# Layer 0's values by conjugate symmetry (264 real columns for 512), and layer 1 rebuilt with packed, transposed k

## The chip, the cores and the metric

The kernel runs on one core of one Trainium2 chip. A core has a matrix engine (PE, with its weight loads shown apart as PEld), a vector engine (DVE), an activation engine (ACT), a general engine (POOL) and queues for DMA; each works through its own instructions in its own order, and semaphores tie them together. The metric is device time in microseconds (us), the median of several runs. A matmul keeps one operand (the weights, `lhsT`) in the array and streams the columns of the other; a float32 matmul shows as two passes in the trace, each with its own weight load.

## The reference, cut to what matters

The input is 8 images of 256 channels, 96 x 96 pixels. Two layers follow each other, each added to its own input after a group norm (`_gn`).

```python
# layer 0: 8 heads of 32 channels
q_f, k_f, v_f = fft2(W1 x + b1), fft2(W2 x + b2), fft2(W3 x + b3)
q_f, k_f = l2_normalize(q_f), l2_normalize(k_f)
attn = einsum('bhcn,bhdn->bhcd', q_f, k_f) * temperature
attn = complex(softmax(real(attn)), softmax(imag(attn)))
out = abs(ifft2(einsum('bhcd,bhdn->bhcn', attn, v_f)))
x = x + W_out out
# layer 1: linear attention, d = 32
q = softplus(Wq xf + bq);  k = softplus(Wk xf + bk);  v = Wv xf + bv
attn_map = einsum('bdn,ben->bde', k, v)
k_sum = sum_n k + 1e-6
out = einsum('bnd,bde,bn->ben', q, attn_map, 1 / einsum('bnd,bd->bn', q, k_sum))
x = x + out
```

In the kernel the attention, the 2D transforms and W3 of layer 0 are folded together: each image row h is multiplied by a small complex matrix per batch (`mz`), giving a complex value z per pixel and channel, and then by a table T of the row (`tmat`, constant), giving a complex y whose absolute value is what W_out is applied to.

## The kernel before, in words

The eight images (batches) go one after the other. A batch's x is four tiles of 128 partitions x 2 halves of channels x 2304 pixels (24 rows each), taken from a pool of eight such buffers; the same pool gives layer 0's result `rs` (four) and layer 1's `kq` and `ex`. One tile framework records the instructions in program order: every engine keeps that order, and each wait comes from a buffer or a datum. PSUM is split into six banks handed round in a ring (`psum`, `ps_tile`, L70) and two more for sums that stay (`pacc`).

The stages of a batch:

- Statistics of x (`bn_stats`, L148, called at L494), then `group_norm` (L153) and the scaled weights.
- The q and k products of layer 0 (L235, L238), 72 chunks of 128 pixels, with squares on ACT (L243), their sum on POOL (L244) and the logits (L220); then softmax and the table `mz` (L268 to L306), 512 columns wide: 256 real and 256 imaginary parts.
- The z loop (L330 to L345), over 96 rows in pairs (`TR` = 2). For a row, PE makes z (two matmuls of 512 columns, L338), DVE adds the bias row (`zt`, L341), and `column` (L311) of the row before follows: four T products of 192 columns (L316, L318) into one PSUM bank, ACT squares them (L321), DVE adds the squares of real and imaginary parts (L322), and after the second row of a pair ACT takes four roots (L326) into `rs`. T's rows come by a DMA for each pair (L334) on the SP queue.
- W_out (`po`, L356), added to x on DVE (L358), with the statistics of layer 1.
- Layer 1: `kq` (L390) makes k and q for 384 pixels of all four x tiles at once, the four tiles in the four column groups of the array (32 outputs each), so that one PSUM bank holds four tiles' values and the order is half outside, tile inside. Softplus (L177) is Abs, Exp and Ln on ACT with DVE steps between.
- The sums of k and x: for 18 steps i, eight transposes of x (L420), two evictions (L425 on ACT, L427 on DVE), one transpose of k (L429, evicted by ACT at L430), and four `kx` matmuls (L408), one for each x tile, in the four column groups again. Then small matmuls make the table `am` (L443 to L460).
- The output (L463 to L488): for each of six slices of 384 pixels a denominator (L466), its reciprocal (L468, DVE) and a product (L469, POOL), made one slice ahead; then for each half of the channels four `o` matmuls (L481), one for each x tile, with 32 rows of weights each in the four row groups, and four adds to x (L484). An output DMA of 384 KB goes out for each tile and slice (L486). The next batch's x comes by four DMAs: two at the start of layer 1 (L383), one after the sums (L439), and one after the output (L488), since a buffer must be free for each.

Of the kernel before, what the change touches and what calls it, by code (L numbers as in the profile page):

```python
# [25 lines left out]
F32 = mybir.dt.float32  # L27
# [4 lines left out]
P = 128  # L32
KC = 2
# [4 lines left out]
TR = 2  # L38
GN_EPS = 1e-5
# [5 lines left out]
def two_layer_kernel(ctx: ExitStack, tc: tile.TileContext, x, w1t, b1, w2t, b2, w3, b3, wot, temp,  # L45
# [8 lines left out]
    SW = 768  # L54
    NS = TW // CH
    XW = XR * W
    assert C == KC * P and NT == 4 and TW % CH == 0 and XW % P == 0 and TW % SW == 0 and SW % P == 0 and ROWS % TR == 0
# [6 lines left out]
    psum = ctx.enter_context(tc.tile_pool(name="psum", bufs=6, space=bass.MemoryType.PSUM))  # L64
# [25 lines left out]
    e0blk = const.tile([P, P], F32, name="e0blk")  # L90
    nc.vector.memset(e0blk, 0.0)
    for j in range(4):
        s = slice(32 * j, 32 * j + 32)
        nc.vector.memset(hblk[s, s], 1.0)
        nc.vector.memset(e0blk[s, 32 * j:32 * j + 1], 1.0 / HEAD)
    rep4 = const.tile([P, P], F32, name="rep4")
    nc.vector.reduce_sum(rep4[:, 0:D], ident.rearrange("p (j d) -> p d j", d=D), axis=AX.X)
    for j in range(1, 4):
        nc.vector.tensor_copy(rep4[:, 32 * j:32 * j + 32], rep4[:, 0:D])
    xT = const.tile([P, 4, 2, C + 2], F32, name="xT")  # L100
    nc.vector.memset(xT, 1.0)
# [3 lines left out]
    nc.scalar.dma_start(out=gri, in_=gmat)  # L105
    epsb = const.tile([P, 1], F32, name="epsb")
# [8 lines left out]
    nc.scalar.dma_start(out=wo, in_=wot.rearrange("(k p) o -> p k o", p=P))  # L115
# [10 lines left out]
    nc.scalar.dma_start(out=bvrow, in_=bv.partition_broadcast(P))  # L126
    b3col = const.tile([P, KC], F32, name="b3col")
    for k in range(KC):
        nc.scalar.dma_start(out=b3col[:, k:k + 1], in_=b3[k * P:(k + 1) * P].unsqueeze(1))
    bkq4 = const.tile([P, 2], F32, name="bkq4")  # L130
    for j in range(4):
        nc.scalar.dma_start(out=bkq4[32 * j:32 * j + 32, 0:1], in_=bk.unsqueeze(1))
        nc.scalar.dma_start(out=bkq4[32 * j:32 * j + 32, 1:2], in_=bq.unsqueeze(1))
# [43 lines left out]
    def softplus(z, e, name):  # L177

        u = two.tile([P, SW], F32, tag="xf", name=f"spu_{name}")
        nc.vector.tensor_scalar_add(u, e, 1.0)  # L180
        nc.vector.scalar_tensor_tensor(e, in0=u, scalar=1.0, in1=e, op0=ALU.subtract, op1=ALU.subtract)
        nc.scalar.activation(u, u, AF.Ln)
        nc.vector.tensor_sub(u, u, e)
        nc.vector.scalar_tensor_tensor(z, in0=z, scalar=0.0, in1=u, op0=ALU.max, op1=ALU.add)  # L184
# [17 lines left out]
    def layer0(b, st0):  # L202
# [13 lines left out]
        lg = [pacc.tile([P, 512], F32, tag="acc", name=f"lg{m}_{b}") for m in range(KC)]  # L216
# [51 lines left out]
        mz = one.tile([P, KC, 2 * C], F32, tag="wbig", name=f"mz_{b}")  # L268
        pz = ps_tile(f"zb_{b}")
        for m in range(KC):  # L270
# [16 lines left out]
            nc.tensor.matmul(pa[:, 0:2 * P], lhsT=sbd, rhs=gri, start=True, stop=True)  # L287
            at = one.tile([P, 2, P], F32, tag="at", name=f"at_{b}_{m}")
            nc.scalar.copy(at[:, 0, :], pa[:, 0:P])
            nc.vector.tensor_add(at[:, 1, :], e0blk, pa[:, P:2 * P])  # L290
            for c in range(2):
                cols = slice(c * C + m * P, c * C + (m + 1) * P)
                nc.tensor.matmul(pz[:, cols], lhsT=b3b[:, m, :], rhs=at[:, c, :], start=True, stop=True)
            for k in range(KC):
                pm = ps_tile(f"mz_{b}_{m}_{k}")
                nc.tensor.matmul(pm[:, 0:2 * P], lhsT=w3n[:, m, k * P:(k + 1) * P],
                                 rhs=at.rearrange("p c o -> p (c o)"), start=True, stop=True)
                for c in range(2):
                    nc.vector.tensor_scalar_mul(mz[:, k, c * C + m * P:c * C + (m + 1) * P],
                                                pm[:, c * P:(c + 1) * P], rstd[:, k:k + 1])  # L300
        zrow = one.tile([P, 2 * C], F32, tag="row", name=f"zrow_{b}")
        nc.scalar.copy(zrow, pz)
        pn = ps_tile(f"zm_{b}")
        for k in range(KC):
            nc.tensor.matmul(pn, lhsT=nmb[:, k, :], rhs=mz[:, k, :], start=(k == 0), stop=(k == KC - 1))
        nc.vector.tensor_add(zrow, zrow, pn)  # L306
# [4 lines left out]
        def column(h, zt, tm, s2):  # L311
            hl = h % TR
            py = ps_tile(f"y_{b}_{h}")
            for m in range(KC):
                o = slice(m * 2 * W, (m + 1) * 2 * W)
                nc.tensor.matmul(py[:, o], lhsT=zt[:, m * P:(m + 1) * P], rhs=tm[:, hl, W:3 * W],  # L316
                                 start=True, stop=False)
                nc.tensor.matmul(py[:, o], lhsT=zt[:, C + m * P:C + (m + 1) * P], rhs=tm[:, hl, 0:2 * W],  # L318
                                 start=False, stop=True)
            sq = two.tile([P, KC, 2, W], F32, tag="sq", name=f"ysq_{b}_{h}")  # L320
            nc.scalar.activation(sq.rearrange("p m c w -> p (m c w)"), py[:, 0:KC * 2 * W], AF.Square)  # L321
            nc.vector.tensor_add(s2[:, :, :, hl], sq[:, :, 0, :], sq[:, :, 1, :])  # L322
            if hl == TR - 1:
                for g in range(NT):
                    r4 = rs[g].rearrange("p k (h w) -> p k h w", w=W)
                    nc.scalar.activation(r4[:, :, :, h - TR + 1:h + 1],  # L326
                                         s2[:, :, g * ROWS:(g + 1) * ROWS, :], AF.Sqrt)

        pending = None
        for h in range(H):  # L330
            g, hl = divmod(h, ROWS)
            if h % TR == 0:
                tm = two.tile([W, TR, 3 * W], F32, tag="xf", name=f"tm_{b}_{h}")
                nc.sync.dma_start(out=tm, in_=tmat[:, h:h + TR, :])  # L334
                s2 = two.tile([P, KC, W, TR], F32, tag="s2", name=f"s2_{b}_{h}")
            ps = ps_tile(f"z_{b}_{h}")
            for k in range(KC):
                nc.tensor.matmul(ps[0:W, :], lhsT=xs[b][g][:, k, hl * W:(hl + 1) * W], rhs=mz[:, k, :],  # L338
                                 start=(k == 0), stop=(k == KC - 1))
            zt = three.tile([W, 2 * C], F32, tag="qk", name=f"zt_{b}_{h}")  # L340
            nc.vector.tensor_add(zt, zrow[0:W, :], ps[0:W, :])  # L341
            if pending is not None:
                column(*pending)
            pending = (h, zt, tm, s2)
# [17 lines left out]
    def layer1(b, st1):  # L362
        nmean, rstd, nmb = group_norm(st1, f"b{b}")
        wkq = one.tile([P, KC, 2, 4, D], F32, tag="row", name=f"wkq_{b}")
        wvs = one.tile([P, KC, C], F32, tag="wbig", name=f"wvs_{b}")
        for k in range(KC):
            for c, w in enumerate((wk, wq)):
                nc.vector.tensor_scalar_mul(wkq[:, k, c], w[:, k, :].unsqueeze(1).to_broadcast([P, 4, D]),
                                            rstd[:, k:k + 1])
            nc.vector.tensor_scalar_mul(wvs[:, k, :], wv[:, k, :], rstd[:, k:k + 1])  # L370
        pb = ps_tile(f"l1b_{b}")
        for c in range(2):
            for k in range(KC):
                nc.tensor.matmul(pb[:, C + c:C + c + 1], lhsT=wkq[:, k, c], rhs=nmean[:, k:k + 1],
                                 start=(k == 0), stop=(k == KC - 1))
# [171 lines left out]
```

## Time and profile before

| what | value |
|---|---|
| median of 3 runs | 5337.23 us (5336.09 to 5342.2) |
| profiled execution | 5342.2 us, span in the trace 5340.2 us |
| PE, DVE, ACT, POOL busy | 4945.2, 2533.8, 1402.8, 966.2 us |
| a batch (second: from its bias row to that of the next) | 714.57 to 1379.19, 664.6 us |
| of it: q, k products, softmax, `mz` | 714.57 to 895.40, 180.8 us |
| z loop | 895.40 to 1186.66, 291.3 us |
| `po`, group norm, layer 1's weights | 1186.66 to 1259.85, 73.2 us |
| in the first batch: k, q columns and sums | 594.8 to 648.4, 53.6 us |
| its output | 652.33 to 692.71, 40.4 us |

A profile row names the line, the engine, the operation, output and inputs, the count, the busy time and the mean length of one in ns, and the time for which the engine was idle before such an instruction, with what ended it. Busy times are summed for each engine and overlap between engines, so that what bounds a stage is read from that stage alone: from the chain of waits, and from the timeline in which starts repeat. The clock column (PEclk) is the share of full speed that PE was granted. Some costly rows:

```profile
L338 PE MATMUL z<-mz,x 128*96 128x512 f32 x3072 | 1444.0, 592 | 0.0
L341 DVE TENSOR_TENSOR zt<-zrow,z 96x512 f32<-96x512 f32 x768 | 524.7, 683 | 599.3 <-PE z L338 599.3
L321 ACT ACTIVATE ysq<-y 128x384 f32<-128x384 f32 x768 | 376.3, 490 | 1498.2 <-PE y L318 1498.2
L148 DVE BATCH_NORM_STATS2 st<-x 128x6 f32<-128x384 f32 x768 | 393.5, 554 | 51.9 <-DMA x<-in_x_dram 45.9
```

ACT's wait for y in the z loop (1498.2 us in all) shows that it has room there; DVE's waits for z say the same.

### The profile page before, as it was taken

The numbers are of one execution on the slowest core, as the hardware profiler recorded it, in microseconds if no ns is written. First come the engines' busy times: TensorE is split into PE (matmuls) and PEld (weight loads), VectorE is DVE, ScalarE is ACT, GpSimd is POOL, SyncE is SP. The second block draws the span as 40 slices with busy tenths as digits, with TensorE's granted clock in tenths as the row PEclk, the third lists the DMA queues.
The fourth block names the chain that finished last, engine by engine and source line by source line (L and its number), as shares of the span: only waits on it lengthen the run. The fifth ranks groups of instructions, "written<-read, shape, count | busy, mean of one in ns | idle before, by whom it ended". The sixth has DMA issues, their size and how long they took to land.

```text
span 5340.2 us, 61775 instructions
## 1 busy us (share of the span) xinstructions
PE 4945.2 (93%) x23024; PEld 3423.1 (64%) x23024; DVE 2533.8 (47%) x4724; ACT 1402.8 (26%) x3576; POOL 966.2 (18%) x1102
## 2 busy tenths in 40 slices
PE   6999989999899998999989999899998999889998
PEld 5766567665676647766477664776647766476664
DVE  4333843338433484334843348433483334833347
ACT  1222212222122221222222222222222222222222
POOL 4400044000430005300053000530005300052000
PEclk9999989998899988999889998899988999899997
DMA  2011120111101111011110112101121011200101
GB/s 86 12 37 32 66 77 13 38 31 71 72 14 37 36 72 66 16 37 47 71 54 17 38 45 74 51 17 37 45 83 42 19 37 56 82 30 21 37 24 72
DMA packets 107914, 241.89 MB, mean 45 GB/s; under 512 B 11488, under 2 KB 62560, under 8 KB 99424
## 3 DMA queue, kind: packets, MB, share of 16 engines
q1 hardware_dynamic: 103936, 235.97, 13.3%
q8 instruction: 184, 3.01, 0.2%
q10 hardware_dynamic: 3680, 1.97, 0.1%
q14 instruction: 114, 0.93, 0.1%
HBM read 162.40 MB, written 75.50 MB: 45 GB/s over the span
## 4 chain that ended last, share of the span: by engine, by line
PE 88%; DVE 6%; ACT 3%; DMA 2%; issue 1%; POOL 0%; SPq 0%; ACTq 0%; DVEq 0%; POOLq 0%
PE z L338 25%; PE qk L235 9%; PE y L316 9%; PE y L318 9%; PE qk L238 9%; PE po L356 9%; PE lg L220 5%; PE o L481 3%; PE xT L420 3%; DVE st L148 2%; PE kx L408 2%; DMA x<-in_x_dram 1%; PE kq L390 1%; DVE x L484 1%; PE den L466 1%
## 5 line engine op out<-in xcount | busy, mean ns | idle before, releaser
L338 PE MATMUL z<-mz,x 128*96 128x512 f32 x3072 | 1444.0, 592 | 0.0
L244 POOL TENSOR_TENSOR acc<-acc,sq 128x512 f32<-128x512 f32 x576 | 730.3, 1268 | 477.2 <-ACT sq L243 474.9
L341 DVE TENSOR_TENSOR zt<-zrow,z 96x512 f32<-96x512 f32 x768 | 524.7, 683 | 599.3 <-PE z L338 599.3
L316 PEld LDWEIGHTS y<-tm,zt 96*128 96x128 f32 x3072 | 562.5, 190 | 384.4 <-issue 380.1
L241 DVE TENSOR_TENSOR qks<-brow,qk 128x512 f32<-128x512 f32 x576 | 396.2, 688 | 851.8 <-PE qk L238 851.8
L321 ACT ACTIVATE ysq<-y 128x384 f32<-128x384 f32 x768 | 376.3, 490 | 1498.2 <-PE y L318 1498.2
L338 PEld LDWEIGHTS z<-mz,x 128*96 128x96 f32 x3072 | 499.6, 163 | 419.6 <-issue 417.7
L316 PE MATMUL y<-tm,zt 96*128 96x192 f32 x3072 | 751.2, 326 | 0.0
L318 PE MATMUL y<-tm,zt 96*128 96x192 f32 x3072 | 748.8, 325 | 0.0
L322 DVE TENSOR_TENSOR s<-ysq 128x192 f32<-128x192 f32 x768 | 277.2, 361 | 919.6 <-ACT ysq L321 919.6
L243 ACT ACTIVATE sq<-qks 128x512 f32<-128x512 f32 x576 | 363.5, 631 | 931.5 <-DVE qks L241 929.7
L235 PE MATMUL qk<-w12s,x 128*128 128x256 f32 x2304 | 594.8, 381 | 0.0
L238 PE MATMUL qk<-w12s,xf 128*128 128x256 f32 x2304 | 592.1, 379 | 0.0
L318 PEld LDWEIGHTS y<-tm,zt 96*128 96x128 f32 x3072 | 539.2, 189 | 0.0
L194 POOL COPY xf<-x 128x190 f32<-128x190 f32 x32 | 10.9, 342 | 2866.4 <-DVE kq L184 2858.7
L356 PE MATMUL po<-r,wo 128*128 128x384 f32 x1536 | 497.5, 487 | 10.8 <-ACT r L326 10.8
L238 PEld LDWEIGHTS qk<-w12s,xf 128*128 128x128 f32 x2304 | 438.7, 190 | 60.0
L356 PEld LDWEIGHTS po<-r,wo 128*128 128x128 f32 x1536 | 291.2, 190 | 214.6 <-ACT r L326 13.2
L235 PEld LDWEIGHTS qk<-w12s,x 128*128 128x128 f32 x2304 | 397.3, 192 | 37.9 <-issue 7.5
L148 DVE BATCH_NORM_STATS2 st<-x 128x6 f32<-128x384 f32 x768 | 393.5, 554 | 51.9 <-DMA x<-in_x_dram 45.9
L220 PEld LDWEIGHTS lg<-qks 128*128 128x128 f32 x2304 | 347.1, 191 | 34.1 <-DVE qks L241 4.8
L220 PE MATMUL lg<-qks 128*128 128x128 f32 x2304 | 350.8, 275 | 3.2 <-DVE qks L241 3.2
(140 smaller groups left out, 3367.4 us busy)
## 6 DMA issues: line engine op xcount, KB each, us to landing
tm<-in_tmat_dram SPq DMA_DIRECT2D x384, 216.0 KB, 2.6
x<-in_x_dram SPq DMA_DIRECT2D x32, 2304.0 KB, 8.1
out_dram<-x SPq DMA_DIRECT2D x192, 384.0 KB, 3.7
w<-in_w1t_dram ACTq DMA_DIRECT2D x1, 256.0 KB, 8.6
w<-in_w2t_dram ACTq DMA_DIRECT2D x1, 256.0 KB, 8.9
w3n<-in_w_dram ACTq DMA_DIRECT2D x1, 256.0 KB, 9.0
wo<-in_wot_dram ACTq DMA_DIRECT2D x1, 256.0 KB, 9.2
wv<-in_wvt_dram ACTq DMA_DIRECT2D x1, 256.0 KB, 9.6
```

The costliest lines, as they stand in the source:

```text
L148: nc.vector.bn_stats(out=st[:, k, g * NS + s, :], in_=xt[:, k, s * CH:(s + 1) * CH])
L220: nc.tensor.matmul(lg[m][:, 0:P], lhsT=qk[:, m * P:(m + 1) * P], rhs=qk[:, C + m * P:C + (m + 1) * P], start=(i == 0), stop=(i == NT * NI ...
L235: nc.tensor.matmul(ps[:, 0:C], lhsT=xg[:, k, n], rhs=w12s[:, k, 0:C], start=(k == 0), stop=(k == KC - 1))
L238: nc.tensor.matmul(ps[:, C:2 * C], lhsT=xf[:, k, nf], rhs=w12s[:, k, C:2 * C], start=(k == 0), stop=(k == KC - 1))
L241: nc.vector.tensor_add(qk, brow, ps)
L244: nc.gpsimd.tensor_add(acc, acc, sq)
L316: nc.tensor.matmul(py[:, o], lhsT=zt[:, m * P:(m + 1) * P], rhs=tm[:, hl, W:3 * W], start=True, stop=False)
L318: nc.tensor.matmul(py[:, o], lhsT=zt[:, C + m * P:C + (m + 1) * P], rhs=tm[:, hl, 0:2 * W], start=False, stop=True)
L321: nc.scalar.activation(sq.rearrange("p m c w -> p (m c w)"), py[:, 0:KC * 2 * W], AF.Square)
L338: nc.tensor.matmul(ps[0:W, :], lhsT=xs[b][g][:, k, hl * W:(hl + 1) * W], rhs=mz[:, k, :], start=(k == 0), stop=(k == KC - 1))
L341: nc.vector.tensor_add(zt, zrow[0:W, :], ps[0:W, :])
L356: nc.tensor.matmul(po[:, 0:CH], lhsT=wo[:, k, m * P:(m + 1) * P], rhs=rs[g][:, k, n], start=(k == 0), stop=(k == KC - 1))
```

## The change

Layer 0: the values of a head's channels are conjugates of each other in pairs, n and 32 - n, so that 17 of 32 channels determine all. `mz` gets 33 x 8 = 264 real columns (17 real and 16 imaginary parts of channel values times 8 heads) for 512. A row then needs three T products instead of four: of the first 128 columns with the one part of T, of the second 128 with the turned part, and of 8 columns (the channels that have no partner) apart. The sum and the difference of the first two give the pair's two values; so there is a copy by ACT (`yb`), an add and a subtraction by DVE (`yc`), a square of 768 values by ACT, a square of 8 x 384 (`x2`), two adds on POOL and the four roots, all once for a pair of rows. `wo` is loaded in the matching order of channels by 32 small DMAs on SP.

PSUM: the ring has four banks instead of six, and the staying tiles have two banks each instead of one.

Layer 1: k is made pixel by pixel (`k_group`: 12 chunks of 128 pixels as weights, 32 columns streamed), q as before but with the tile outside and the half inside (`q_chunk`); the sums go over 72 chunks of 128 pixels (`kx_group`), each with two transposes, one eviction on DVE, and one matmul into the same 32 rows. The softplus takes 384 columns at a time. `wvs` and `bvs` are gone: the scale goes into `kxT`. Output: all six denominators first, then tile by tile, one DMA of a whole x tile (2304 KB) for each. Layer 1 holds one x buffer instead of two, so that three loads of the next x are issued at its start and the fourth after the first output tile.

```diff
+NZ = 33
+NH = 8
-    psum = ctx.enter_context(tc.tile_pool(name="psum", bufs=6, space=bass.MemoryType.PSUM))
+    psum = ctx.enter_context(tc.tile_pool(name="psum", bufs=4, space=bass.MemoryType.PSUM))
     pacc = ctx.enter_context(tc.tile_pool(name="pacc", bufs=2, space=bass.MemoryType.PSUM))
...
-    nc.scalar.dma_start(out=wo, in_=wot.rearrange("(k p) o -> p k o", p=P))
+    wo_v = wot.rearrange("(n q) o -> q n o", q=HEAD)
+    for j in range(16):
+        for k in range(KC):
+            c = (j, HEAD - j if j else 16)[k]
+            nc.sync.dma_start(out=wo[8 * j:8 * j + 8, k, :], in_=wo_v[c])
...
-    def softplus(z, e, name):
-        u = two.tile([P, SW], F32, tag="xf", name=f"spu_{name}")
+    def softplus(dst, z, name):
+        e = two.tile([P, CH], F32, tag="sq", name=f"spe_{name}")
+        nc.scalar.activation(e, z, AF.Abs)
+        nc.scalar.activation(e, e, AF.Exp, scale=-1.0)
+        u = two.tile([P, CH], F32, tag="s2", name=f"spu_{name}")
...
-            sq = two.tile([P, KC, 2, W], F32, tag="sq", name=f"ysq_{b}_{h}")
-            nc.scalar.activation(sq.rearrange("p m c w -> p (m c w)"), py[:, 0:KC * 2 * W], AF.Square)
-            nc.vector.tensor_add(s2[:, :, :, hl], sq[:, :, 0, :], sq[:, :, 1, :])
+            real, turned = tm[:, hl, W:3 * W], tm[:, hl, 0:2 * W]
+            nc.tensor.matmul(py[:, hl, 0:2 * W], lhsT=zt[:, 0:P], rhs=real, start=True, stop=True)
+            nc.tensor.matmul(py[:, hl, 2 * W:4 * W], lhsT=zt[:, P:2 * P], rhs=turned, start=True, stop=True)
+            nc.tensor.matmul(px[0:NH, hl * 2 * W:(hl + 1) * 2 * W], lhsT=zt[:, 2 * P:2 * P + NH], rhs=real,
+                             start=True, stop=True)
+            if hl < TR - 1:
+                return
+            yb = two.tile([P, TR, 2 * W], F32, tag="sq", name=f"yb_{b}_{h}")
+            nc.scalar.copy(yb, py[:, :, 2 * W:4 * W])
+            yc = two.tile([P, KC, TR, 2 * W], F32, tag="xf", name=f"yc_{b}_{h}")
+            nc.vector.tensor_add(yc[:, 0], py[:, :, 0:2 * W], yb)
+            nc.vector.tensor_sub(yc[:, 1], py[:, :, 0:2 * W], yb)
+            x2 = one.tile([NH, TR, 2 * W], F32, tag="x2", name=f"x2_{b}_{h}")
+            nc.scalar.activation(x2.rearrange("p t w -> p (t w)"), px[0:NH, 0:TR * 2 * W], AF.Square)
+            yf = yc.rearrange("p k t w -> p (k t w)")
+            nc.scalar.activation(yf, yf, AF.Square)
+            s2 = two.tile([P, KC, W, TR], F32, tag="s2", name=f"s2_{b}_{h}")
+            s2t = s2.rearrange("p k w t -> p k t w")
+            nc.gpsimd.tensor_add(s2t, yc[:, :, :, 0:W], yc[:, :, :, W:2 * W])
+            nc.gpsimd.tensor_add(s2t[0:NH, 1], x2[:, :, 0:W], x2[:, :, W:2 * W])
+            for g in range(NT):
+                r4 = rs[g].rearrange("p k (h w) -> p k h w", w=W)
+                nc.scalar.activation(r4[:, :, :, h - TR + 1:h + 1], s2[:, :, g * ROWS:(g + 1) * ROWS, :], AF.Sqrt)
...
-            zt = three.tile([W, 2 * C], F32, tag="qk", name=f"zt_{b}_{h}")
+            zt = three.tile([W, NZ * NH], F32, tag="qk", name=f"zt_{b}_{h}")
...
-        kq = x_tile(f"kq_{b}")
-        ex = x_tile(f"ex_{b}")
+        qp = x_tile(f"qp_{b}").rearrange("p k n -> p (k n)")
         if b + 1 < B:
-            xs[b + 1] = [load_x(b + 1, g) for g in range(NT - 2)]
+            xs[b + 1] = [load_x(b + 1, g) for g in range(NT - 1)]
...
+        def q_chunk(s):
+            n = slice(s * CH, (s + 1) * CH)
+            ps = ps_tile(f"q_{b}_{s}")
+            for j in range(NT):
+                for k in range(KC):
+                    nc.tensor.matmul(ps[32 * j:32 * j + 32, 0:CH], lhsT=wq4s[:, k, j, :],
+                                     rhs=xs[b][j][:, k, n], start=(k == 0), stop=(k == KC - 1))
+            z = three.tile([P, CH], F32, tag="qk", name=f"zq_{b}_{s}")
+            nc.vector.tensor_scalar_add(z, ps[:, 0:CH], bqs)
+            softplus(qp[:, n], z, f"q{b}_{s}")
...
+        def k_group(t):
+            ps = ps_tile(f"k_{b}_{t}")
+            for i in range(KG):
+                for k in range(KC):
+                    nc.tensor.matmul(ps[:, i * D:(i + 1) * D], lhsT=x_chunk(t * KG + i, k), rhs=wks[:, k, :],
+                                     start=(k == 0), stop=(k == KC - 1))
+            z = three.tile([P, KG, D], F32, tag="qk", name=f"zk_{b}_{t}")
+            nc.vector.tensor_add(z, ps[:, 0:KG * D].rearrange("p (i d) -> p i d", d=D),
+                                 bks.unsqueeze(1).to_broadcast([P, KG, D]))
+            sp = two.tile([P, KG * D], F32, tag="xf", name=f"spk_{b}_{t}")
+            softplus(sp, z.rearrange("p i d -> p (i d)"), f"k{b}_{t}")
+            return sp
...
+        def kx_group(t, ks):
+            pend = None
+            for c in range(t * KG, (t + 1) * KG):
+                pt = ps_tile(f"xT_{b}_{c}")
+                for k in range(KC):
+                    nc.tensor.transpose(pt[:, k * P:(k + 1) * P], x_chunk(c, k), ident)
+                xt = three.tile([P, C + 1], F32, tag="qk", name=f"xt_{b}_{c}")
+                nc.gpsimd.memset(xt[:, C:C + 1], 1.0)
+                nc.vector.tensor_add(xt[:, 0:C], nmrow, pt[:, 0:C])
+                if pend is not None:
+                    add_kx(*pend)
+                pend = (ks, c, xt)
+            add_kx(*pend)
         pend = None
-        for t in range(TW // SW):
...
+        for t in range(NG):
+            ks = k_group(t)
+            q_chunk(t)
+            if pend is not None:
+                kx_group(*pend)
+            pend = (t, ks)
+        kx_group(*pend)
...
-        normalize(0)
-        for s in range(NS):
...
+        for g in range(NT):
+            xg = xs[b][g]
+            jj = slice(32 * g, 32 * g + 32)
+            for s in range(NS):
+                n = slice(s * CH, (s + 1) * CH)
+                for m in range(KC):
+                    ps = ps_tile(f"o_{b}_{g}_{s}_{m}")
+                    nc.tensor.matmul(ps[:, 0:CH], lhsT=am[jj, m * P:(m + 1) * P], rhs=qp[jj, n],
+                                     start=True, stop=True)
+                    nc.vector.tensor_add(xg[:, m, n], xg[:, m, n], ps[:, 0:CH])
+            nc.sync.dma_start(out=out_v[b, :, :, g * TW:(g + 1) * TW], in_=xg)
+            if g == 0 and b + 1 < B:
+                xs[b + 1].append(load_x(b + 1, NT - 1))
```

## The prediction

> **What bounds the kernel now.** I read the page's shares first, then the chain that ended last, the costliest groups, the windows by stage, and the timeline where the change lands. The chain says TensorE: 88% of the span, z and y (L316, L318, L338) alone 43%.
>
> ```profile
> PE 4945.2 (93%) x23024; PEld 3423.1 (64%) x23024; DVE 2533.8 (47%) x4724; ACT 1402.8 (26%) x3576; POOL 966.2 (18%) x1102
> PE 88%; DVE 6%; ACT 3%; DMA 2%; issue 1%; POOL 0%; SPq 0%; ACTq 0%; DVEq 0%; POOLq 0%
> ```
>
> The z loop's timeline (start, length, engine) shows how it goes:
>
> ```profile
> 319.56 1.88 PE L338 MATMUL z<-mz,x 128*96 128x512 f32 x4
> 319.82 0.49 ACT L321 ACTIVATE ysq<-y 128x384 f32<-128x384 f32 x1 [1.30 <-PE y L318]
> 320.34 0.36 DVE L322 TENSOR_TENSOR s<-ysq 128x192 f32<-128x192 f32 x1 [1.20 <-ACT ysq L321]
> 322.57 1.88 PE L338 MATMUL z<-mz,x 128*96 128x512 f32 x4
> 323.75 0.80 ACT L326 ACTIVATE r<-s 128x96 f32<-128x96 f32 x4 [0.43 <-DVE s L322]
> ```
>
> z starts repeat every 3.01 us (322.57 - 319.56): a row. Passes follow each other without a gap, and all other engines wait for PE. So cutting columns pays there, until another engine's work per row is longer. Windows by stage of one batch (PE, PEld, DVE, ACT, POOL busy; then clock, DMA share, GB/s):
>
> ```profile
> 595.00:612.00 17.00, 17.00 (x186) 6.32 (x179) 10.56 (x17) 14.16 (x22) 0.00 (x0) 0.92 0.01 1
> 612.00:649.00 37.00, 33.12 (x309) 21.18 (x307) 28.00 (x40) 22.93 (x51) 0.47 (x2) 0.95 0.01 1
> 656.00:693.00 37.00, 35.41 (x104) 18.20 (x104) 33.88 (x54) 0.00 (x0) 5.01 (x6) 0.50 0.59 214
> 693.00:715.00 22.00, 1.60 (x5) 1.43 (x6) 14.21 (x35) 0.26 (x1) 1.68 (x4) 0.50 0.48 178
> ```
>
> The k and q columns take 17 us, layer 1's sums 37, its output 37. In the output the clock is 0.50 all through, though PE is busy, and DVE is nearly full too. Last, the stretch with no PE work is in the chain:
>
> ```profile
> 694.68 9.60 DMA x<-in_x_dram
> 704.30 5.62 DVE st L148 x12
> ```
>
> The next batch's last x tile is waited for.
>
> **What the Trainium skill says.** "TensorE: Matmul & The Clock Gate", LDWEIGHTS: a weight load takes its columns over 1.2, 107 ns for 128, however few columns are then streamed. The trace agrees: eight transposes of 128 columns start to end in 1.09 us. The same page, Why this matters for your kernels: a matmul of 32 rows takes as long as one of 128, and gains only by running beside others on other row or column groups. The trace has that too: eight kx passes of 257 columns, four groups side by side, take 0.64 us together. The same page, Part 1: an idle window of about 3.4 us halves the clock and a busy one restores it. The first half agrees (0.50 after the reciprocals); the second doesn't hold for the output's 32-row matmuls here, 37 us at 0.50. The same page, Architectural detail: ACT and DVE take their instructions strictly in order; the z loop below rests on that.
>
> **The change part by part** (per batch; there are eight). Durations from the profiled execution: 5342.2 us, span 5340.2; the median of the runs is 5337.23, 5.0 below.
>
> 1. *z loop.* PE: a row had z 2 x 512 and y 4 x 192 columns, 1792 in all for 3.01 us. It has 2 x 264 and 3 x 192, 1104: 1.85 us, 3.71 a pair. If PE stayed the bound, 48 pairs would take 178 instead of 291.3 us (895.40 to 1186.66 in the chain). But the rest is now one chain, from the copy of a pair to that of the next, since ACT holds yb, x2, the square, four roots, then the next yb, in this order:
>  - ACT yb, 128x384 out of PSUM: 0.49 (row L321), hop 0.09 (above, ACT's end at 320.31 to DVE's start is 0.03; from DVE to POOL at the reciprocals 0.14; I take values between);
>  - DVE add and sub of 384 with PSUM: 1.02 (two of 0.46 to 0.55, rows L358 and L484);
>  - ACT square of 768 in SBUF: 0.85 (row L182), hops 0.09;
>  - POOL add of 384: 1.00 (row L469, 996 ns), hop 0.05;
>  - POOL add of 192 on 8 partitions: 0.59 (from L469 and L244, 996 ns for 384 and 1268 for 512 elements, 2.1 ns an element), hop 0.05;
>  - ACT four roots: 0.80.
>  Sum about 4.97 us. 48 pairs and some 4 us of ends: 242.6, so **-48.7**. The bounds: 4.6 (smaller DVE and POOL pieces) to 5.6 (POOL's add writes every second element, which no row shows; DVE's zt adds of about 0.4 get in between yb and yc). PE is then busy 75% of a pair, and waits in slices below 2 us, so I leave its clock at full. tm's buffer and load are beside all this; x2 lies beside DVE's two adds.
>
> 2. *Table mz.* Half the columns in matmuls and evictions, two DVE multiplies for four, one add for copy and add, in a serial stage: about 4 us of small steps go, **-4**. The start's 32 small wo loads go ahead of tm on SP, but lie beside the first qk stage, 180 us: 0.
>
> 3. *Layer 1's sums.* Removed: kq with k, 16.5 us, and 18 steps of 1.70 (636.66, 638.36, 640.06 in the trace), with the first softplus 53.6 in batch 0 and 51.2 in batch 1; I take 52. Added:
>  - k_group, six times: 12 chunks x 2 halves of x as weights, two passes each: 48 loads of 128 columns, at 0.109 us (the transposes' 1.09 over 10, 8 on average 0.136): 5.2; only 32 columns are streamed on each;
>  - q_chunk, six times: 8 matmuls of 384 columns. Two halves of one group follow each other, so it is between 1.3 (four groups side by side) and 5.1 (none): 3.2;
>  - 72 chunks: two transposes 0.22 to 0.33, kx with one group of 32 columns, two passes of 257 columns in sequence at full clock 0.43 to 0.48, 0.1 between kinds: 0.87. Before, the four groups of kx were side by side: 0.64 for four chunks, now 4 x 0.48. DVE's 0.41 (256 columns from PSUM) and POOL's one-column memset are below it.
>  One period is 5.2 + 3.2 + 12 x 0.87 + about 1.3 of softplus in the way (xt shares three buffers with zk and zq) = 20.1. First k and q and second k 13.6, four periods of 20.1 and a last stretch of 26 (a q, two kx groups, pauses) make 120; 4 more for the last softplus's latency make 124, so **+72**. Bounds +50 (q side by side, chunks at 0.75) to +95 (k_group at half clock in part, since it streams a quarter of the time; softplus, 12 of 384 with two table loads of 1.28 each, not covered). ACT and DVE have room in the mean: 12 x (0.9 of ACT and 1.8 of DVE) and the loads are below 10 us a period.
>
> 4. *Output.* Before, 652.33 to 692.71, 40.4 us, DVE's: 6 reciprocals of 2.5 and 48 adds of 0.467; the o matmuls of four groups went side by side, in the trace same-group passes 0.64 apart at half clock (1.28 a matmul). Now all reciprocals stand first in DVE's queue (15 us; only the four o's that PSUM holds are done by then), and the matmuls go group by group, each by itself: 44 x 1.28 = 56.3 at half clock. 71.5 for 40.4, **+31**. At full clock 44 x 0.64 = 28 makes 44 to 46, +4 to +5. I take half clock: that stage never left 0.50 before, with more of the array in use.
>
> 5. *Ends.* The fourth x load is issued after the first quarter's output, some 50 us ahead of need, and three others early enough for their statistics to fall into other stages: the wait of 9.60 goes, and about 2 of statistics: **-11.6**, in seven batches. What is late next is the last tile's statistics, DVE after its adds. The last output DMA, 2304 KB for 384, ends about 4 us later, once. wvs and bvs gone, kxT scaled instead: 0.
>
> Sum: 8 x (-48.7 - 4 + 72 + 31) - 7 x 11.6 + 4 = **+325**: 5667 on the profiled execution, 5662 on the median.
>
> **The rivals.**
>  (a) *The output runs at full clock.* For it: PE has no pause there now, and single matmuls fill time. Against: windows of 0.50 with PE busy 35.4 of 37 us. 26 less a batch, 208: about 5454. Still slower.
>  (b) *The other side, faster: the z loop runs at PE's pace.* One mechanism, in the loop, if POOL's and DVE's links are shorter than their rows. PE's 3.71 a pair for 4.97 gives 60 a batch, 480: about 5180. It decides from 4.1 us a pair (325 over 8 over 48 is 0.85). For it: POOL's second add touches 8 partitions, and no row shows such an add. Against: without that add the chain is still 4.3, and ACT's order leaves no overlap of pairs.
>  (c) *Layer 1 loses the clock.* k_group streams a quarter of the time, and the softplus stalls add pauses; parts of the sums at half clock cost some 25 more a batch: about 5860.
>
> **How the numbers follow.** The forecast 0.54, own range 5560 to 5760; (a) 0.18; (b) 0.12; (c) 0.16. The range 5390 to 5880 leaves out (b) and the worse half of (c). A difference of 0.2%, 11 us, is about what can be told from none: it has only the seam between (a) and (b), 0.02. Faster 0.11, slower 0.87. The predicted time is 5660.
>
> **What would show it.** Right: ACT's yb every 5 us, with PE waiting for zt or yb; POOL's two adds 1.6 in each pair; po, the qk stage as before; 120 us from the first k to the last kx, kx passes with no overlap; output matmuls 1.28 apart at clock 0.50, 70 us; no wait for x before the next statistics. Wrong: pairs at 3.7 to 4.1 us; output matmuls 0.64 apart; q's groups side by side and chunks at 0.7; clocks of 0.5 in the sums.

## The result, and the profile after

The changed kernel takes 5785.76 us (median of 4 runs, 5783.51 to 5793.86), the kernel before 5339.33 beside it: 1.084 times as long, with an interval of 1.082 to 1.0858. The profiled execution's span is 5792.0 us for 5340.2.

The page's shares and chain of the kernel after:

```profile
PE 5220.6 (90%) x22832; PEld 3441.6 (59%) x22832; DVE 2544.9 (44%) x5336; ACT 1605.0 (28%) x3752; POOL 1631.8 (28%) x2446
PE 73%; DVE 13%; ACT 8%; issue 4%; POOL 1%; DMA 0%; DVEq 0%; ACTq 0%; POOLq 0%
```

The chain's second line is what to read: PE had 88% of it and has 73%; DVE and ACT have 21% for 9%. DMA, 2% before, is gone. But PE's busy time is longer than before (5220.6 for 4945.2), though z's passes have fewer columns and y's passes are fewer. It must have grown elsewhere. Stage by stage, from the first and last instructions of each in the two traces (means over eight batches; the sums run from the first product of k or q to the last kx):

| stage | before | after | difference | foreseen |
|---|---|---|---|---|
| q, k, softmax, mz | 179.3 | 177.8 | -1.5 | -4 |
| z loop | 291.4 | 238.5 | -52.9 | -48.7 |
| po | 62.2 | 64.4 | +2.2 | 0 |
| group norm, weights of layer 1 | 6.5 | 9.0 | +2.4 | 0 |
| layer 1's k, q and sums | 57.9 | 148.0 | +90.1 | +72 |
| small matmuls after | 4.0 | 3.4 | -0.6 | 0 |
| output | 39.1 | 65.5 | +26.4 | +31 |
| to the next batch | 20.8 | 10.5 | -10.3 | -10 (7 of 8) |

The sum is 55.9 us a batch, 447 in all; with 4.8 us of later start it is the 452 by which the span grew. The z loop gains what was foreseen, and layer 1 loses more than twice that.

The z loop after, one pair in the timeline (start, length, engine; only ACT, DVE's yc and POOL):

```profile
1795.94 0.46 ACT L340 COPY yb<-y 128x384 f32<-128x384 f32 x1
1796.50 0.56 DVE L342 TENSOR_TENSOR yc<-y,yb 128x384 f32<-128x384 f32 x1 [2.21 <-ACT yb L340]
1796.97 0.55 DVE L343 TENSOR_TENSOR yc<-y,yb 128x384 f32<-128x384 f32 x1
1797.55 0.84 ACT L347 ACTIVATE yc<-yc 128x768 f32<-128x768 f32 x1 [0.78 <-DVE yc L343]
1798.47 0.99 POOL L350 TENSOR_TENSOR s<-yc 128x384 f32<-128x384 f32 x1 [3.28 <-ACT yc L347]
1799.55 0.58 POOL L351 TENSOR_TENSOR s<-x 8x192 f32<-8x192 f32 x1
1800.16 0.81 ACT L354 ACTIVATE r<-s 128x96 f32<-128x96 f32 x4 [1.77 <-POOL s L351]
1800.88 0.46 ACT L340 COPY yb<-y 128x384 f32<-128x384 f32 x1
```

From one copy to the next, each line starts within 0.1 us of the end of the one above it: 1800.88 - 1795.94 = 4.94 us a pair. PE waits in this loop now, before the first product of a row, for DVE's `zt` (140.7 us in all in the page's row of L333).

Two windows of the second layer after, the first group of k and q, and the output (columns as before: PE, PEld, DVE, ACT, POOL busy, then clock, DMA share, GB/s):

```profile
1991.00:2008.00 17.00, 17.00 (x99) 14.85 (x98) 4.67 (x11) 4.67 (x6) 0.00 (x0) 0.60 0.00 1
2152.00:2203.00 51.00, 50.73 (x90) 26.94 (x90) 25.20 (x48) 0.00 (x0) 2.66 (x5) 0.50 0.46 186
```

PE counts as busy all through both, and has 0.60 and 0.50 of its clock. In the first, almost all that it does is k's passes, 48 of them in 10.43 us, each with a weight load of 128 columns and 32 columns streamed:

```profile
1991.31 10.43 PE L441 MATMUL k<-wks,x 128*128 128x32 f32 x48
2001.67 2.81 PE L427 MATMUL q<-x,wq4s 128*32 128x384 f32 x16
2004.41 7.34 PE L441 MATMUL k<-wks,x 128*128 128x32 f32 x48
```

### The profile page after: what moved, and what is told of

The parts are those of the page before. It is cut to its first block, busy times and chain, and to the rows that moved or that the text cites. A ratio compares the mean times of both kernels' runs of the same rounds, so it can differ in the third digit from the quotient of the medians.

```text
span 5792.0 us, 63110 instructions
## 1 busy us (share of the span) xinstructions
PE 5220.6 (90%) x22832; PEld 3441.6 (59%) x22832; DVE 2544.9 (44%) x5336; ACT 1605.0 (28%) x3752; POOL 1631.8 (28%) x2446
## 3 DMA queue, kind: packets, MB, share of 16 engines
q14 instruction: 127, 1.04, 0.1%
## 4 chain that ended last, share of the span: by engine, by line
PE 73%; DVE 13%; ACT 8%; issue 4%; POOL 1%; DMA 0%; DVEq 0%; ACTq 0%; POOLq 0%
PE qk L254 9%; PE qk L257 9%; PE z L366 8%; PE po L384 8%; PE o L521 7%; PE k L441 6%; PE kx L452 5%; PE lg L239 4%; PE y L333 4%; ACT r L354 4%; PE y L335 3%; DVE yc L343 3%; PE xT L460 2%; PE y L334 2%; ACT yb L340 2%
## 5 line engine op out<-in xcount | busy, mean ns | idle before, releaser
L366 PE MATMUL z<-mz,x 128*96 128x264 f32 x3072 | 868.1, 406 | 0.0
L350 POOL TENSOR_TENSOR s<-yc 128x384 f32<-128x384 f32 x384 | 382.1, 995 | 1304.1 <-ACT yc L347 1304.1
L342 DVE TENSOR_TENSOR yc<-y,yb 128x384 f32<-128x384 f32 x384 | 214.1, 558 | 1128.8 <-ACT yb L340 1117.1
L384 PE MATMUL po<-r,wo 128*128 128x384 f32 x1536 | 515.2, 499 | 38.4 <-ACT r L354 38.4
L333 PE MATMUL y<-tm,zt 96*128 96x192 f32 x1536 | 410.7, 348 | 140.7 <-DVE zt L369 140.7
L354 ACT ACTIVATE r<-s 128x96 f32<-128x96 f32 x1536 | 309.9, 276 | 644.7 <-POOL s L351 644.7
L521 PE MATMUL o<-qp,am 32*128 32x384 f32 x768 | 445.4, 853 | 30.0 <-DVE rec L510 30.0
L452 PE MATMUL kx<-xt,spk 128*32 128x257 f32 x1152 | 389.9, 436 | 77.2 <-DVE xt L463 75.9
L333 PEld LDWEIGHTS y<-tm,zt 96*128 96x128 f32 x1536 | 264.4, 189 | 327.8 <-DVE zt L369 288.8
L347 ACT ACTIVATE yc<-yc 128x768 f32<-128x768 f32 x384 | 324.0, 844 | 285.1 <-DVE yc L343 285.1
L441 PEld LDWEIGHTS k<-wks,x 128*128 128x128 f32 x2304 | 360.9, 250 | 36.4 <-issue 23.1
```

The costliest lines, as they stand in the source:

```text
L333: nc.tensor.matmul(py[:, hl, 0:2 * W], lhsT=zt[:, 0:P], rhs=real, start=True, stop=True)
L354: nc.scalar.activation(r4[:, :, :, h - TR + 1:h + 1], s2[:, :, g * ROWS:(g + 1) * ROWS, :], AF.Sqrt)
L366: nc.tensor.matmul(ps[0:W, 0:NZ * NH], lhsT=xs[b][g][:, k, hl * W:(hl + 1) * W], rhs=mz[:, k, :], start=(k == 0), stop=(k == KC - 1))
L384: nc.tensor.matmul(po[:, 0:CH], lhsT=wo[:, k, m * P:(m + 1) * P], rhs=rs[g][:, k, n], start=(k == 0), stop=(k == KC - 1))
L441: nc.tensor.matmul(ps[:, i * D:(i + 1) * D], lhsT=x_chunk(t * KG + i, k), rhs=wks[:, k, :], start=(k == 0), stop=(k == KC - 1))
L452: nc.tensor.matmul(kx[0:D, 0:C + 1], lhsT=ks[:, i * D:(i + 1) * D], rhs=xt, start=(c == 0), stop=(c == NG * KG - 1))
```

## The experiments

Times are medians, each beside runs of the kernel before on the same chip (5339 to 5344 us).

**1. The roots later in ACT's order.**

```diff
-            for g in range(NT):
-                nc.scalar.activation(r4..., AF.Sqrt)
+            if late:
+                roots(*late.pop())
+            late.append((h, s2))
```

> The changed kernel with one edit: the four roots of a pair of rows are issued on ACT after the next pair's copy, x2 and square instead of before them. Theory (the pair's time is a chain through ACT's order: copy, DVE, square, POOL, roots, next copy): the chain is cut, the pair falls from 4.97 us to PE's 3.7 to 3.9, the z loop from 238.5 to about 185 us, the whole by 8 x 53, to about 5360. Rival 1 (POOL's two adds or DVE are simply too slow for the rate, or PE streams slower than worked out): the loop stays above 225. Rival 2 (the two PSUM tiles of y are what holds PE back): it stays at 238.

5785.34 us, ratio 1.0822 (1.08 to 1.0844); z loop 238.1 to 238.8. Its timeline shows why nothing moved:

```profile
1796.62 0.58 POOL L351 TENSOR_TENSOR s<-x 8x192 f32<-8x192 f32 x1
1797.23 0.80 ACT L359 ACTIVATE r<-s 128x96 f32<-128x96 f32 x4 [1.77 <-POOL s L351]
1797.94 0.46 ACT L340 COPY yb<-y 128x384 f32<-128x384 f32 x1
```

The roots still wait for the POOL add that has just ended and still stand ahead of the next copy: the order in the trace isn't the one written. The loop's first instructions on ACT show it best: one root of the first pair, at 242.46 us, stands ahead of the second pair's copy, at 242.65, where the program now has none. So an engine's order isn't always the program's, unlike what the description of the kernel before says of the framework. This run tells nothing of the chain, and the order had to be changed through data.

**2. Layer 0 new, layer 1 old.**

The layer's whole text is that of the kernel before; against that kernel, two of the lines that fit it to the new PSUM:

```diff
-    psum = ctx.enter_context(tc.tile_pool(name="psum", bufs=6, space=bass.MemoryType.PSUM))
+    psum = ctx.enter_context(tc.tile_pool(name="psum", bufs=4, space=bass.MemoryType.PSUM))
...
-        kx = pacc.tile([P, 512], F32, tag="acc", name=f"kx_{b}")
+        kx = pacc.tile([P, 2, 512], F32, tag="acc", name=f"kx_{b}")[:, 0, :]
```

> Layer 0 of the changed kernel with layer 1, output and loads of the kernel before (its buffers refitted to the four PSUM banks of the ring). Theory (layer 0 gains some 50 us a batch, and all that is lost is lost in layer 1's sums and output): about 5339 - 8 x 53 = 4915, the sums back at 58 to 62 us, the output at 39 to 45 (four banks instead of six may slow it), the tail of 22.7 back. Rival (the ring of four banks or the new memory layout costs layer 1 its time, not the new sums): sums and output stay well above those of the kernel before, 5200 or more.

4978.79 us, ratio 0.9317 (0.9302 to 0.9333). z loop 238, sums 57.6 to 60.1, output 46.5, tail 21.2. The sums' loss is the new layer 1's own and not that of the ring of four banks. The old output takes some 7 us a batch more than in the kernel before, which is most of what this run lacks to the 4915 foreseen. That the ring is the reason fits run 8, where half of the output uses other banks and the loss is gone.

**3. q's matmuls between those of k.**

```diff
             for i in range(KG):
+                if i % 3 != 2:
+                    q_mm(pq, t, *todo.pop(0))
                 for k in range(KC):
```

> The changed kernel with q's eight matmuls of a group put between k's chunks instead of after them: same instructions, other order. Theory (k_group streams 32 columns for each 128-column weight load, so PE counts as a quarter busy, and the clock falls to half in it): with q's 384 columns in between, the clock stays full, 48 weight loads take 5.2 us in every group instead of 5.2 to 10.4, the sums of 142 to 155 us become 125 to 138 and equal in all batches; 5786 - 8 x 14 = about 5670. Rival (the clock isn't what stretches k): no change, within 20 us, the clock in the first groups stays at 0.5.

6169.47 us, ratio 1.1548 (1.1531 to 1.1565): 384 us slower, sums at 194 to 196. Both theories missed. The window in which layer 1 of the second batch starts, in this kernel:

```profile
1309.00:1353.00 44.00, 44.00 (x123) 23.36 (x123) 5.04 (x13) 4.55 (x6) 0.00 (x0) 0.50 0.00 0
```

For 44 us PE is never idle and never gets above half clock. Summed over a batch, from each start on PE to the next one, q takes 46.6 us for 16.4, k 47.4 for 45.6, and the transposes and kx 102 for 86. The first is because q's column groups no longer run side by side: a matmul by itself, two passes, takes 1.41 us from its start to the next one at this clock, where eight took 2.81 in all. Why the last grew stays open. So q's columns between those of k don't bring the clock back. Whether the clock is what stretches k, this run doesn't show; run 9 does.

**4. The old order of the output.**

```diff
-        for g in range(NT):
-            for s in range(NS):
-                for m in range(KC):
+        for s in range(NS):
+            for m in range(KC):
+                for j in range(NT):
```

> The changed kernel with the output in the old order: slice outside, the four x tiles inside, so that four o matmuls of 32 rows follow each other in four row groups; output DMAs for each slice, the last x load after them. The six denominators stay ahead of it. Theory (o matmuls of one row group follow each other at half clock, 1.13 to 1.28 us each): the output falls from 65.5 to 39 to 44 us, now DVE's 15 + 48 x 0.467; the tail rises from 10.8 to about 22, since the x load is waited for again; sum about -12 a batch, 5690. Rival (the reciprocals ahead of it, or four banks, are what costs): the output stays above 55 us.

5675.05 us, ratio 1.0621 (1.0605 to 1.0637). Output 41.5 for 65.5, tail 21.5 for 10.8. A window of its output, in the same columns as above:

```profile
2142.00:2150.00 8.00, 8.00 (x30) 6.37 (x27) 7.03 (x15) 0.00 (x0) 0.00 (x0) 0.50 0.98 351
```

The clock is 0.50 here too, but 30 passes take 8 us, where the changed kernel has 90 in 51. So the output's loss is that matmuls of one row group follow each other; the six reciprocals ahead and four banks together cost 2.4 us over the kernel before.

**5. One add on POOL.** ACT copies the 8 rows into yc before the square, so POOL's second add isn't needed; DVE's subtraction moves ahead of its addition, so that this copy needn't wait for both:

```diff
-            nc.scalar.activation(x2..., px[0:NH, 0:TR * 2 * W], AF.Square)
-            nc.gpsimd.tensor_add(s2t[0:NH, 1], x2[:, :, 0:W], x2[:, :, W:2 * W])
+            nc.scalar.copy(yc[0:NH, 1]..., px[0:NH, 0:TR * 2 * W])
```

> The changed kernel's z loop without POOL's second add: ACT copies the 8 rows of px into yc before the square, in place of squaring them into x2, so that the one POOL add of 384 takes them along; DVE's subtraction comes before its addition. Theory (a pair's time is the chain copy, DVE, square, POOL, roots, next copy, since the roots of a pair still stand before the next copy on ACT): the add of 0.58 us and its hop leave the chain, the pair falls from 4.93 to 4.3 to 4.4 us, the z loop from 238.5 to 210 to 217, the whole from 5786 to about 5580. Rival (PE's passes or the PSUM tiles of y set the pace, and POOL lies beside them): the z loop stays above 233.

5625.33 us, ratio 1.0528 (1.0511 to 1.0546); z loop 217.0 to 218.3. 21 us for 48 pairs, 0.44 us each, against 0.6 by the chain alone. So POOL's add was on the path. About 0.1 of what is missing is ACT's copy, which now stands in the chain: in the timeline the square starts 1.71 us after the pair's first copy (1792.39 - 1790.68), 1.61 before (1797.55 - 1795.94).

**6. Roots once for two pairs**, on top of that:

```diff
-            for g in range(NT):
+            if u == 0:
+                return
+            for g in range(NT):
```

> As the kernel without POOL's second add, and the roots taken once for two pairs (four rows), so that in every second pair no roots and no POOL stand between a square and the next copy. Theory (the chain through POOL and roots is what is left above PE's 3.7 us a pair): 3.8 to 4.1 us a pair, the z loop 185 to 200, the whole about 5430 to 5480. Rival (PE or DVE is the bound from 4.4 us on): no faster than the kernel without the second add.

5567.27 us, ratio 1.0421 (1.04 to 1.0442); z loop 208.7 to 209.4, 4.3 us a pair, neither the 3.8 to 4.1 nor the rival's standstill. PE's lines in its timeline:

```profile
1792.19 1.13 PE L370 MATMUL z<-mz,x 128*96 128x264 f32 x4
1793.16 0.49 PE L333 MATMUL y<-tm,zt 96*128 96x192 f32 x2
1793.48 0.49 PE L334 MATMUL y<-tm,zt 96*128 96x192 f32 x2
1793.90 0.49 PE L335 MATMUL y<-tm,zt 96*8 96x192 f32 x2
1794.33 1.13 PE L370 MATMUL z<-mz,x 128*96 128x264 f32 x4
```

No wait is named on any of them, so PE is the bound, at 2.14 us a row (1794.33 - 1792.19), where the columns make 1.85. The starts tell where the rest is: L333 to L334 is 0.32, the two passes of 192 columns; L334 to L335 is 0.42 and L335 to z 0.43. Around the product with 8 columns of weights PE pauses by 0.1 each time, and z's first pass takes 0.08 longer than the others. That the 8 columns are the reason is tested in the next run.

**7. That product with 128 columns.** z's columns in another order, in the mix of run 8 (below):

```diff
-            nc.tensor.matmul(px[0:NH, ...], lhsT=zt[:, 2 * P:2 * P + NH], rhs=real,
+            nc.tensor.matmul(px[:, ...], lhsT=zt[:, 0:P], rhs=real,
```

> The mix with layer 0 of the changed kernel, one POOL add, roots for four rows and the old layer 1 (4707 us), with the columns of z in another order, so that the third T product takes 128 columns as weights (8 of use, 120 that another product has already) instead of 8. Theory (in that mix PE is the bound of the z loop, at 2.13 us a row, of which some 0.27 are three pauses of 0.08 to 0.09 where the tile of the array changes between 8 and 128 columns): the pauses go, though 120 more columns are loaded; a row takes 1.86 to 1.95 us, the z loop falls from 209 to 184 to 194, the whole to 4530 to 4590. Rival (the pauses come from the semaphores or the streaming of 192 columns, or the chain of ACT, DVE and POOL already needs 4.2 us a pair): within 4 us of 209.

4540.19 us, ratio 0.8501 (0.8489 to 0.8514); z loop 187.8 to 188.8 for 209. The timeline:

```profile
1449.90 1.06 PE L368 MATMUL z<-mz,x 128*96 128x264 f32 x4
1450.80 0.49 PE L331 MATMUL y<-tm,zt 96*128 96x192 f32 x2
1451.13 0.49 PE L332 MATMUL y<-tm,zt 96*128 96x192 f32 x2
1451.45 0.49 PE L333 MATMUL y<-tm,zt 96*128 96x192 f32 x2
1451.78 1.06 PE L368 MATMUL z<-mz,x 128*96 128x264 f32 x4
```

All three products are 0.32 to 0.33 apart now. With 120 more columns of weights, 120 of its 128 results unused, the product is cheaper. A row takes 1.88 us here (1451.78 - 1449.90), 3.76 a pair; the loop's 188 us are 3.92 a pair, so that part of the chain is felt again.

**8. The mix**: layer 0 as in run 6, layer 1 old, the output's first half of the channels in the four staying banks.

```diff
+                    if m == 0:
+                        if j % 2 == 0:
+                            pp = pacc.tile([P, 2, 512], F32, tag="acc", name=f"o_{b}_{s}_{j}")
+                        ps = pp[:, j % 2, :]
```

> Layer 0 of the changed kernel with one POOL add and roots for four rows, layer 1 of the kernel before with x transposed into buffers shared with T's rows, and the output's first half of the channels in the four staying PSUM banks. If the z loop follows the chain: 190 to 200 us in it, sums 58 to 62, output 39 to 43; 4979 - 8 x 48 = about 4600. If the z loop is bound by something else than the chain from 4.4 us on: about 4790.

4707.26 us, ratio 0.8815 (0.8802 to 0.8829): z loop 209, sums 57.6 to 59.9, output 38.5 to 39.4. It lies between the two values foreseen, since the z loop had PE's 4.3 us as its next bound.

**9. Four times the columns in k.**

```diff
-                    nc.tensor.matmul(ps[:, i * D:(i + 1) * D], ..., rhs=wks[:, k, :],
+                    nc.tensor.matmul(ps[:, i * D:(i + 4) * D], ..., rhs=wks[:, k, :, :],
```

> The changed kernel with four times the columns streamed in k_group: 128 for 32 on each weight load, the surplus overwritten by the next chunk; more work for PE, the same result. Theory (the clock falls to half in k_group because PE streams a quarter of the time there): the clock stays or comes back at full, a k_group takes 5.2 to 6 us instead of up to 10.4, the sums fall from 142 to 155 us to 128 to 140; the whole to 5690 to 5740. Rival (the clock isn't set by how much is streamed, or streaming costs what it saves): sums as before or longer by up to 30 us.

5675.46 us, ratio 1.0627 (1.0611 to 1.0643); sums 130 to 131 in all batches. The fourth group of k and q of one batch (two more passes of k stand ahead of it, before a kx), and two windows of that batch's sums:

```profile
2008.56 5.40 PE L442 MATMUL k<-wks,x 128*128 128x128 f32 x46
2013.89 1.52 PE L428 MATMUL q<-x,wq4s 128*32 128x384 f32 x16
1962.00:1974.00 12.00, 9.66 (x78) 7.02 (x77) 7.50 (x16) 9.51 (x14) 0.20 (x2) 0.98 0.01 1
1975.00:2095.00 120.00, 102.71 (x548) 53.23 (x548) 55.15 (x124) 24.18 (x34) 8.83 (x73) 0.94 0.00 1
```

Before the edit, the 48 passes of a group took 5.9 to 10.05 us from the first start to the last, and q 2.81; the clock, 0.98 and 0.94 in these windows, was 0.60 in the window shown above and 0.78 to 0.92 in the four windows of 24 us behind that. More streaming takes less time, and q, which wasn't touched, halves too: it had run at half clock behind k. Of the 17 us a batch, by the starts on PE, 10 are k's (35.6 for 45.6) and 8 q's (8.7 for 16.4); transposes and kx take 87 for 86. This shows that k's thin streaming held the clock down. In a batch's first group it didn't make it fall: there (third batch of the changed kernel) the clock is 0.50 before k begins, from 1987.5 to 1991.0 in the small products of the group norm, and stays so for all of k, while in this run it is back 3 us after k's start.

**10. The sums in pairs of chunks**, on top of run 9:

```diff
+            for u in range(2):
+                i = c % KG + u
+                nc.tensor.matmul(kx[D * u:D * u + D, 0:C + 1], lhsT=ks[:, i * D:(i + 1) * D], rhs=xt[:, u, :],
```

> As the changed kernel with 128 columns streamed in k_group (5675 us, sums 131), and the sums in pairs of chunks: four transposes, one eviction of 512 columns, and two kx matmuls in two column groups of the array. Theory (after the clock, the sums' cost is that each chunk's kx runs alone in 32 columns of the array, 0.62 us in a chunk of 0.92): 36 pairs of 1.35 to 1.5 instead of 1.83 us, the sums at 113 to 120, the whole at 5560 to 5590. Rival (evictions behind softplus on DVE and the buffers of xt set the pace): sums 125 or more.

5410.84 us, ratio 1.0134 (1.0117 to 1.0151); sums 99 to 101, 31 less where 11 to 18 were foreseen. Two chunks' kx go side by side in the time of one:

```profile
1955.91 0.63 PE L456 MATMUL kx<-xt,spk 128*32 128x257 f32 x4 [0.23 <-DVE xt L468]
1956.47 0.66 PE L465 MATMUL xT<-ident,x 128*128 128x128 f32 x4
```

Four passes in 0.63; after the edit there are also half as many evictions on DVE and half as many changes between transposes and kx. By the starts on PE, kx takes 21 us a batch for 43, the transposes with the waits behind them 33 for 44, and k 2 more. The first is the passes side by side; what the fewer evictions and changes are worth apart from it, no run shows.

**11. q in the old order.**

```diff
-            for j in range(NT):
-                for k in range(KC):
+            for k in range(KC):
+                for j in range(NT):
```

> The changed kernel with q's eight matmuls in the old order, half outside and tile inside, so that all four column groups run side by side. Plain sum: a group's q falls from 2.81 to about 1.4 us, the sums by 8 us, the whole to about 5720. Rival (q's dense stretch is what brings the clock back after a k_group; a shorter one brings it back less often): the sums stay or grow, and more k_groups run at 0.5.

5777.64 us, ratio 1.0822 (1.0806 to 1.0838); sums 142 to 149. No change, as the rival said, but for another reason: q's four groups ran side by side already. In the trace of the changed kernel, the first passes of all four start within 0.04 us, with 0.61 to 0.64 us to the next four, which is 384 columns at half clock.

## Why the prediction was right, and where its terms were off

Slower was right, and the measured 5786 lies in the range (5390 to 5880), 125 us above the forecast of 5660. But it is above the forecast's own range (5560 to 5760) and nearer to rival (c), 5860; of its signs of being wrong, clocks of 0.5 in the sums came, and q's groups side by side, though with chunks of 0.92 us and not 0.7. The direction was right for the reason given, that layer 1 loses more than the z loop gains. That the number isn't further off owes something to chance, since terms that were too low and too high met in it. The steps, in their order:

- **z loop: right.** Foreseen 4.97 us a pair through ACT, DVE and POOL (the links as listed add up to 5.03), measured 4.94, and run 5 shows that POOL's second add was in the chain; that add, which no row had shown, took 0.58 for 0.59. What was wrong here is PE's own need, 3.71 us a pair: it left out the pauses around the 8-column product and is 4.27 (run 6). So rival (b), PE's pace from 3.71, could not have come about in this kernel; even without the chain the loop would have stopped at 209 us.
- **mz: -1.5 for -4.** Small; the runs don't show which step gave less.
- **Layer 1's sums: the mis-sized term.** Foreseen 124 us, measured 142 to 156, mean 148. By the starts on PE, k takes 45.6 us a batch for 31.2 (six times 5.2), q 16.4 for 19.2 (six times 3.2), and transposes and kx 86 for the 74 that are left.
 - k: "48 loads of 128 columns, at 0.109 us: 5.2" is what the full clock gives, where starts are 0.112 apart with 32 columns streamed as with 128 (run 9: 5.40 for 46 passes). At half clock they are 0.214 apart, and most groups had that clock in part. Run 9 takes 10 of the 14 us off.
 - q: its four groups ran side by side in the changed kernel already (run 11). At half clock that is 2.7 us a time, at full clock 1.45, both below the 3.2. This too high a term hid a part of the loss.
 - Transposes and kx: a regular chunk takes 0.92 us, not 0.87, 4 us in 72. The rest is waits and passes at half clock, not split further. The page has kx wait 77.2 us in all, 9.6 a batch, for the evictions of DVE, which does softplus meanwhile:

```profile
L452 PE MATMUL kx<-xt,spk 128*32 128x257 f32 x1152 | 389.9, 436 | 77.2 <-DVE xt L463 75.9
```

 Of the bounds, "k_group at half clock in part" named the first; rival (c), priced at 25 us a batch and given 0.16, came about in the sums to two thirds (17, run 9). Run 10 shows the other part that was right in kind: kx alone in one column group. The stage before was put at 52 and is 57.9: the first products begin 4 us earlier in the trace, and the last kx of the second batch ends at 1313.6, which makes 53.8 from 1259.85 and not 51.2. This offset 6 of the 24 us by luck.
- **Output: +26.4 for +31.** The clock stayed at 0.50 with PE busy 50.73 of 51 us, and one o took 1.28 us, as foreseen; rival (a) didn't happen. The difference is at the changes from one x tile to the next:

```profile
2161.31 0.56 DVE L523 TENSOR_TENSOR x<-x,o 128x384 f32<-128x384 f32 x1 [0.73 <-PE o L521]
2162.59 0.56 DVE L523 TENSOR_TENSOR x<-x,o 128x384 f32<-128x384 f32 x1 [0.73 <-PE o L521]
2163.87 2.00 DVE L523 TENSOR_TENSOR x<-x,o 128x384 f32<-128x384 f32 x4 [0.72 <-PE o L521]
```

 An add comes every 1.28 us, and then four at once (x4): there, two matmuls of the next row group had run beside the last two of this group (their eight passes start between 2161.07 and 2163.16, where one by one they would take twice that). From one such change to the next it is 12.97 us in this trace, for 12 matmuls that would take 15.36 one by one; three changes save 7 us.
- **Ends: right.** The wait for x is gone, -10.3 a batch in the mean.
- **Terms put at nothing:** po +2.2 and group norm +2.4 a batch and 4.8 at the start, 42 us in all. po's wait for the last roots has grown from 1.35 to 4.8 us a batch, as the idle times of the two pages' rows show (10.8 and 38.4 over eight), and behind it the first six to nine steps between po's passes take 0.5 to 0.8 us instead of 0.32: PE starts at half clock.

```profile
L356 PE MATMUL po<-r,wo 128*128 128x384 f32 x1536 | 497.5, 487 | 10.8 <-ACT r L326 10.8
L384 PE MATMUL po<-r,wo 128*128 128x384 f32 x1536 | 515.2, 499 | 38.4 <-ACT r L354 38.4
```

 After the group norm, the products for the biases and for the row of means stand between k's scaled weights and the first k, 1988.73 to 1991.31; before, the first product of kq came 0.5 us after the first of them. At the start, DVE's multiplication of `tcol` stands until 34.14 us instead of 31.61 waiting for small loads, with 36 statistics of the first batch behind it instead of 31; the profile names one of wo's 32 loads, put at 0 in the prediction, as what ended that wait. No run separates it.

In one sum: (18 for the sums, which are the 24 less the 6 of the stage before, + 4.6 for po and norm + 2.5 for mz - 4.6 for the output - 4.2 for the z loop - 0.6) x 8 is 126, the 127 between 325 and 452.

## What to carry to other kernels

When PE's columns are cut, work out the longest loop through the other engines' queues for one iteration: it is the new bound, and here it let 53 of the 113 us a batch through that the columns promised. A matmul that streams few columns for a full weight load is paid twice, by its own time and by the clock, for itself and for what follows (10 and 8 us a batch, run 9). One that uses one row or column group alone loses the passes that the old form had side by side (24 us a batch of the output, run 4; pairs alone gave 22 of kx back, run 10): count these before such a rebuild. The two halves of a change are worth trying apart: layer 0's new form with the old layer 1, its chain shortened and its third product at 128 columns, is 15% faster than the kernel before.

## What the runs showed of the hardware

- PE paused by about 0.1 us before and after a product with 8 columns of weights (0.42 to 0.43 between starts for 0.32, run 6), and the first pass of z behind it was 0.08 longer; with 128 columns, 120 of them unused, it was quicker (188 us for 209 in the loop, run 7). The change between y's 128 and z's 96 columns cost no such pause there (0.33 from 1451.45 to 1451.78).
- A busy PE wasn't enough for the clock. 48 passes of k with 128 columns of weights and 32 streamed ran at half clock for 10 us with no idle time; with 128 streamed the clock came back within a batch's first group, and later groups ran at full (46 in 5.40, run 9). The output's 32-row matmuls stayed at 0.50 for 51 us of almost unbroken work (50.73 busy), and the mix of k and q in run 3 for 44.
- Passes of four column groups started within 0.04 us of each other though the program puts two matmuls of the same group behind each other (run 11). Whether PE or the framework, which reorders in run 1, brings that about isn't shown.
